# Second pass of a two-layer convolution block: spread and next normaliser placed behind the output projection, scaling of the query weights placed behind the filter's products

## The chip, the cores and the metric

The kernel runs on one core of a Trainium2 chip. The time is the device time of one execution in microseconds; the figure for the kernel before is the median of three runs. A profile is one further execution, recorded by the hardware profiler, with an own time and an own span. The engines are called as the profile calls them: PE (TensorE's matrix products), PEld (its weight loads), DVE (VectorE), ACT (ScalarE), POOL (GpSimd) and SP (SyncE, which here issues DMA transfers).

## The reference

The input x holds 8 images of 384 channels and 64 x 64 points. Two layers follow one another; each normalises over 32 groups of channels and adds its result to x. Cut to what matters:

```python
# layer 0: linear attention over the 4096 points of an image
q = apply_rope_2d(conv1x1(x, Wq, bq))
k = apply_rope_2d(conv1x1(x, Wk, bk))
v = conv1x1(x, Wv, bv)
q = elu(to_heads(q) * scale) + 1.0
k = elu(to_heads(k)) + 1.0
kv = einsum('bhnd,bhne->bhde', k, v)
k_sum = k.sum(axis=2)
normalizer = einsum('bhnd,bhd->bhn', q, k_sum)[..., None]
out = einsum('bhnd,bhde->bhne', q, kv) / (normalizer + 1e-06)
x = x + conv1x1(out, Wfc, bfc)            # of _gn(x)
# layer 1: filter in frequency space on 8x8 blocks, 3x3 depthwise, gate
t = einsum('bchw,oc->bohw', x, w_in)
t = irfft2(rfft2(blocks(t)) * fft_filter)
t = depthwise3x3(t, w_dw)
x = x + einsum('bchw,oc->bohw', gelu(t1) * t2, w_out)   # of _gn(x)
```

All sums are in 32-bit floating point.

## The kernel before

An image is cut into 8 bands of 512 points, and its 384 channels into 3 tiles of 128 partitions. An image goes through three passes. In the first, keys and values of all bands are projected and their product is summed. In the second (`queries`), the queries are projected band by band, divided by their normaliser, and multiplied by the product of the summed keys and values with the output weights; the result is added to x. In the third, layer 1 runs band by band, and between its steps the first pass of the next image is done, so that from image 1 on there is no first pass of its own. Part of the last band of layer 1 of one image (its depthwise taps, gate and contraction: `last_band`) runs inside the second pass of the next.

In the second pass a band j has these steps:

- `q_project`: 9 products of 512 columns (L655; the profile counts 18, since each is carried out as two), three for each tile of channels. Then VectorE turns and adds the biases (L667, L682, L684), ScalarE makes a part of the turned copy (L676) and the two functions of the elu (L379, L380), and VectorE ends it (L381). The function stops after each tile's products (`yield`), so that other work can be placed between them.
- `q_normalise`: 12 small products of the band's queries with the summed keys (L693, tile pn), then a chain that gives the divisor in two parts of 16 bits: on VectorE L701, L702 (reciprocal), L707 and L709, on ScalarE the casts L706 before L707 and L708 before L709. Its result is the tile `parts`.
- `q_spread`: 12 small products that spread `parts` over the channels (L717, tile prb) into four tiles, and four multiplications of the queries by them on VectorE (L726).
- `project_out`: 9 products of the queries with the folded weights (L734, tile pf; 18 in the profile), each three followed by an addition to x on VectorE (L738). After that `band_sums` forms the sums for layer 1's normalisation, on ScalarE for all bands but the first (L180, L183).

`queries` fixes the order in which these steps are written down. A scheduler then places each instruction in its engine's queue by that order, by what it depends on and by its own estimates; each engine runs its queue in order. `tc.issue_after(ins)` makes the instructions of its block stand behind `ins` in the queue, where they are on the same engine.

Within the second pass, besides, run: `late`, the rest of the image before (the taps L855 on VectorE, the gate L867 to L872, a small product L1149 whose copy L1153 holds the weights of the late taps, the contraction L888 and L899), and `chain`, which prepares the next image's key weights: its group statistics (L341 to L355 on VectorE, L348 on ScalarE, two transfers on POOL's queue that end in L359), the scaling of wk (L401) and the bias columns (L422, L426, L427).

`Keys.prepare(4)` is written down after band 4's layer 1 work in the third pass. It loads the next image's query weights wq and scales them (`scale_weight`: three instructions L401 of 384 columns on VectorE). In the built queue of the kernel before, these three stand much earlier, near the end of the second pass, between the steps L702 and L709 of band 7's divisor.

`expand_filter` is the part of layer 1 with the filter: after its products (L766) VectorE multiplies by the filter (L774, tile tf).

The lines that the change touches in `queries`, before:

```python
q_spread(b, j, q[j], normaliser.pop(j))          # j = 2 ... 7
output_ = project_out(b, j - 1, q.pop(j - 1), mt)
if j == NBAND - 2:
    next(output_)
    normalise(j + 1)
run(output_)
```

Of the kernel before, what the change touches and what calls it, by code (L numbers as in the profile page):

```python
# [15 lines left out]
C = 384  # L16
# [3 lines left out]
NBAND = 8  # L20
# [97 lines left out]
def conv_blocks_kernel(ctx: ExitStack, tc: tile.TileContext, a: dict, out: bass.AP, nb: int):  # L118
    nc = tc.nc
# [131 lines left out]
    scale = HD ** -0.5  # L251
# [147 lines left out]
    def scale_weight(w, params, factor=1.0):  # L399
        for i in range(CT):  # L400
            nc.vector.tensor_scalar(w[:, i, :], w[:, i, :], params[0][:, i : i + 1], factor, ALU.mult, ALU.mult)  # L401
# [143 lines left out]
    latest = {}  # L545
# [101 lines left out]
    def q_project(b, j, wqs, bias, q):  # L647
        tq = qp.tile([P, 4, BT], F32, tag="turn", name=f"tq_{b}_{j}")
        nc.sync.dma_start(tq, a["tq"][:, j])
        pq = [None] * CT  # L650

        for m in (2, 0, 1):
            p_ = pq[m] = ps_tile(f"pq_{b}_{j}_{m}")
            for t in range(CT):
                nc.tensor.matmul(  # L655
                    p_,
                    wqs[:, t, m * P : (m + 1) * P],
                    xt[b, j][:, t, :],
                    start=(t == 0),
                    stop=(t == CT - 1),  # L660
                )
            yield
        qc = w_tile([P, CT, BT], f"qc_{b}_{j}")
        qs = w_tile([P, CT, BT], f"qs_{b}_{j}")

        def turn(dst, src, m, table):
            nc.vector.scalar_tensor_tensor(dst, src, m, table, ALU.add, ALU.mult)  # L667

        def by_row(ap):
            return ap.rearrange("p (r w) -> p r w", w=W)  # L670

        def columns(ap):
            return ap.unsqueeze(1).to_broadcast([P, 8, W])

        for to, of in (halves, halves[::-1]):
            nc.scalar.activation(qs[to, 2, :], pq[2][of, :], AF.Identity, bias=bias[of, 2:3])  # L676
        turn(by_row(qc[:, 2, :]), by_row(pq[2]), bias[:, 2:3], columns(cq2))
        for m in range(2):
            turn(qc[:, m, :], pq[m], bias[:, m : m + 1], tq[:, 2 * m, :])
            turn(qs[:, 1 - m, :], pq[m], bias[:, m : m + 1], tq[:, 3 - 2 * m, :])  # L680
            if m == 0:
                nc.vector.tensor_mul(by_row(qs[:, 2, :]), by_row(qs[:, 2, :]), columns(sq2))  # L682
        for part in (slice(2, 3), slice(0, 2)):
            nc.vector.tensor_add(qc[:, part], qc[:, part], qs[:, part])  # L684
            elu_plus_one(qc[:, part], qs[:, part])
        q[j] = qc
# [25 lines left out]
    def q_spread(b, j, q, rn):  # L712
        pr = [ps_tile(f"prb_{b}_{j}_{s}") for s in range(4)]
        for t in range(CT):
            for s in range(4):
                strip = slice(32 * s, 32 * s + 32)
                nc.tensor.matmul(  # L717
                    pr[s][:, t * P : (t + 1) * P],
                    expand[strip, t * P : (t + 1) * P],
                    rn[strip, :],  # L720
                    start=True,
                    stop=True,
                )
        for s in range(4):
            qq = q[:, :, s * P : (s + 1) * P]
            nc.vector.tensor_mul(qq, qq, pr[s][:, :C].rearrange("p (t n) -> p t n", t=CT))  # L726
# [3 lines left out]
    def project_out(b, j, q, mt):  # L730
        for m in range(CT):
            p_ = ps_tile(f"pf_{b}_{j}_{m}")
            for t in range(CT):
                nc.tensor.matmul(  # L734
                    p_, mt[:, t, m * P : (m + 1) * P], q[:, t, :], start=(t == 0), stop=(t == CT - 1)
                )
            xm = xt[b, j][:, m, :]
            latest["sum"] = nc.vector.scalar_tensor_tensor(xm, p_, bfc[:, m : m + 1], xm, ALU.add, ALU.add).ins  # L738
            if m == 0:
                yield  # L740
        if j == 1:
            differences[b] = taps_pool.tile([P, CT, BT], F32, tag="dw", name=f"differences_{b}")
        band_sums(b, 1, j, xt[b, j], differences.get(b))


    def expand_filter(b, j, h, done):
        ht = w_tile([P, 4, C], f"ht_{b}_{j}")
        tf = w_tile([P, 4, C], f"tf_{b}_{j}")
        for i in range(4):
            p_ = ps_tile(f"pi_{b}_{j}_{i}")  # L750
            for t in range(CT):
                nc.tensor.matmul(  # L752
                    p_[:, :C],
                    h[:, t, i * P : (i + 1) * P],
                    w_in[:, t, :],
                    start=(t == 0),
                    stop=(t == CT - 1),
                )
            nc.scalar.copy(ht[:, i, :], p_[:, :C])  # L759
        yield  # L760

        for s in range(2):
            p_ = [ps_tile(f"pd_{b}_{j}_{2 * s + i}") for i in range(2)]
            for above in range(2):
                for i in range(2):
                    nc.tensor.matmul(  # L766
                        p_[i][halves[above], :C],
                        dft[halves[i], :],
                        ht[halves[i], 2 * s + above, :],
                        start=True,  # L770
                        stop=True,
                    )
            for i in range(2):
                nc.vector.tensor_mul(tf[:, 2 * s + i, :], p_[i][:, :C], filt)  # L774
        done.append(tf)

    def back_transform(b, j, tf):
# [173 lines left out]
    def run(*chains):  # L951

        chains = list(chains)
        while chains:
            chains = [c for c in chains if next(c, chains) is not chains]

    class Keys:
# [50 lines left out]
        def prepare(self, j):  # L1008

            if self.live and j == 4:  # L1010
                self.wq = load_weight(self.b, "wq", QRUNS)
                if self.b == 0:
                    sum_weight(self.wq, "wq", scale)
                scale_weight(self.wq, self.params, scale)
                if self.b == 0:
                    self.qbias = bias_columns(0, self.params[1], 2 * CT, 3 * CT)
            if self.live and j == NBAND:
                self.wfc = load_weight(self.b, "wfc", k_runs)
                if self.b == 0:
                    self.wv = load_weight(self.b, "wv", k_runs)  # L1020
                    sum_weight(self.wv, "wv")
                    bias_rows(0, bias_columns(0, self.params[1], CT, 2 * CT), CT, self.vbias)

    def queries(b, keys, before_last, late):


        wq, qbias = keys.wq, keys.qbias
        q, done, normaliser = {}, [], {}

        def normalise(j):  # L1030
            normaliser[j] = q_normalise(b, j, q[j])

        run(q_project(b, 0, wq, qbias, q))
        before_last()
        run(keys.accumulate(NBAND - 1))
        next(late, None)
        finish = keys.finish(done)
        for _ in zip(q_project(b, 1, wq, qbias, q), finish):
            pass
        prepared = []  # L1040
        chain = layer0_chain(b + 1, prepared)

        next(late, None)
        normalise(0)
        if b:
            run(finish)
        run(q_project(b, 2, wq, qbias, q))
        run(finish)
        mt = done[0]
        q_spread(b, 0, q[0], normaliser.pop(0))  # L1050
        project = q_project(b, 3, wq, qbias, q)
        next(project)
        normalise(1)
        run(project)
        run(project_out(b, 0, q.pop(0), mt))
        q_spread(b, 1, q[1], normaliser.pop(1))
        normalise(2)
        for j in range(2, NBAND):
            if j < NBAND - 2:
                project = q_project(b, j + 2, wq, qbias, q)  # L1060
                for _ in range(2):
                    next(project)
                normalise(j + 1)
                run(project)
                next(chain, None)
            q_spread(b, j, q[j], normaliser.pop(j))
            output_ = project_out(b, j - 1, q.pop(j - 1), mt)
            if j == NBAND - 2:
                next(output_)
                normalise(j + 1)  # L1070
            run(output_)
            if j < NBAND - 2:
                next(chain, None)
            if j in (5, 7):
                load_x(b + 1, j // 6)
            next(late, None)
        run(chain)
        run(project_out(b, NBAND - 1, q.pop(NBAND - 1), mt))
        return prepared
# [38 lines left out]
    filt = const.tile([P, C], F32, tag="filt", name="filt")  # L1118
# [109 lines left out]
    b = nb - 1  # L1228
# [60 lines left out]
```

## Time and profile before

| what | us |
|---|---|
| median of the runs (lowest, highest) | 3316.01 (3314.86, 3316.93) |
| profiled execution | 3317.55 |
| its span | 3315.8 |
| products L734 pf, 1152 | 510.7 |
| products L655 pq, 1152 | 521.5 |
| taps L855 on DVE, 1401 | 977.5 |
| additions L738 on DVE, 192 | 138.6 |
| granted clock of PE, mean | 0.994 |

The busy shares in the prediction are of the whole span. Where the idle time of an engine was ended by another engine's instruction, the profile names that instruction after an arrow. Lines such as L717 are those of the kernel printed above. Times in a timeline are microseconds from the span's start; an instruction's length contains some 0.08 us in which the next one on VectorE has already begun, so sums over a queue are made from start to start. In the chain of work that ended last, 90% of the span is PE, 5% DVE and 3% ACT.

### The profile page before, as it was taken

To read this page: it belongs to the slowest core of one execution; us is meant where nothing else is said; L and a number is where in the kernel's file an instruction comes from. 1 tells how busy PE (TensorE), PEld (TensorE's weight loads), DVE (VectorE), ACT (ScalarE), POOL (GpSimd) and SP (SyncE) were. 2 spreads that over 40 slices of the span, in tenths; PEclk is the share of its full clock that TensorE was granted. 3 is DMA by queue.
4 is the path that set the end of the run, shared out by engine and by line. 5 is a ranking of instruction groups with operands and counts; after the bars stand their busy time and mean duration, and the time that the engine had idled before them with its cause. 6 is when DMAs were issued, how large, how long until landed. Compare 5 with 4: busy or idle time off the path is not lost.

```text
span 3315.8 us, 53150 instructions
## 1 busy us (share of the span) xinstructions
PE 3256.2 (98%) x21133; PEld 1829.5 (55%) x21133; DVE 2755.8 (83%) x4528; ACT 2020.4 (61%) x4029; POOL 173.7 (5%) x321
## 2 busy tenths in 40 slices
PE   8999999999999999999999999999999999999988
PEld 5544666456664566545665456654566446664454
DVE  6577789978889688896889968998788987889697
ACT  4445666666766566755666656656576665556553
POOL 0000000100010000100001000010000100000000
PEclk9999999999999999999999999999999999999999
DMA  7324334462444523534335433445343551334112
GB/s 217 114 87 117 93 80 117 127 143 68 106 108 127 143 68 96 128 114 127 87 87 137 119 112 77 111 127 118 99 102 91 144 128 52 73 73 126 58 30 48
DMA packets 154446, 346.33 MB, mean 104 GB/s; under 512 B 29813, under 2 KB 41061, under 8 KB 146005
## 3 DMA queue, kind: packets, MB, share of 16 engines
q1 hardware_dynamic: 124500, 282.65, 27.0%
q0 software_dynamic: 29504, 60.06, 12.4%
q8 instruction: 166, 2.72, 0.3%
q14 instruction: 84, 0.68, 0.1%
q10 hardware_dynamic: 192, 0.21, 0.0%
HBM read 235.62 MB, written 99.93 MB: 101 GB/s over the span
## 4 chain that ended last, share of the span: by engine, by line
PE 90%; DVE 5%; ACT 3%; DMA 1%; issue 1%; SPq 0%; DVEq 0%; ACTq 0%
PE pf L734 15%; PE pk L491 14%; PE pi L752 14%; PE pv L507 13%; PE pq L655 13%; PE pw L888 5%; PE pb L787 3%; PE pw L899 3%; PE acc L523 3%; PE pd L766 3%; PE acc L536 2%; DVE dw L855 2%; PE pn L693 1%; ACT mt L570 1%; PE prb L717 1%
## 5 line engine op out<-in xcount | busy, mean ns | idle before, releaser
L855 DVE SCALAR_TENSOR_TENSOR dw<-ring,w_dw,dw 128x512 f32<-128x512 f32 x1401 | 977.5, 746 | 239.9 <-ACT ring L803 200.8
L491 PE MATMUL pk<-wk,x 128*128 128x384 f32 x1536 | 544.9, 496 | 0.0
L655 PE MATMUL pq<-x,wq 128*128 128x512 f32 x1152 | 521.5, 601 | 2.6 <-ACT mt L570 2.6
L752 PE MATMUL pi<-w_in,hf 128*128 128x384 f32 x1536 | 513.5, 491 | 1.3 <-ACT hf L374 1.3
L734 PE MATMUL pf<-qc,mt 128*128 128x512 f32 x1152 | 510.7, 597 | 0.0
L507 PE MATMUL pv<-wv,x 128*128 128x384 f32 x1344 | 470.0, 488 | 0.0
L491 PEld LDWEIGHTS pk<-wk,x 128*128 128x128 f32 x1536 | 283.5, 191 | 205.4 <-issue 32.5
L752 PEld LDWEIGHTS pi<-w_in,hf 128*128 128x128 f32 x1536 | 288.1, 190 | 195.8 <-issue 2.5
L514 ACT COPY v<-pv 128x384 f32<-128x384 f32 x224 | 108.7, 485 | 424.5 <-PE pv L507 423.2
L734 PEld LDWEIGHTS pf<-qc,mt 128*128 128x128 f32 x1152 | 214.3, 190 | 255.5 <-issue 239.6
L507 PEld LDWEIGHTS pv<-wv,x 128*128 128x128 f32 x1344 | 253.6, 190 | 181.4 <-issue 8.4
L655 PEld LDWEIGHTS pq<-x,wq 128*128 128x128 f32 x1152 | 212.8, 190 | 250.6 <-issue 226.2
L738 DVE SCALAR_TENSOR_TENSOR x<-pf,bfc,x 128x512 f32<-128x512 f32 x192 | 138.6, 744 | 81.9 <-PE pf L734 81.4
L379 ACT ACTIVATE qs<-qc 128x512 f32<-128x512 f32 (+1 forms) x128 | 107.0, 836 | 144.2 <-DVE qc L684 143.8
L180 ACT ACTIVATE differences<-x,shift 128x512 f32<-128x512 f32 x168 | 120.0, 714 | 103.8 <-DVE x L738 103.6
L888 PE MATMUL pw<-gated,w_out 128*128 128x256 f32 x768 | 179.3, 383 | 0.0
L494 DVE TENSOR_TENSOR kc<-pk,kvbias 128x384 f32<-128x384 f32 x256 | 140.7, 550 | 40.3 <-PE pk L491 40.2
L759 ACT COPY ht<-pi 128x384 f32<-128x384 f32 x256 | 115.1, 482 | 85.6 <-PE pi L752 81.8
L888 PEld LDWEIGHTS pw<-gated,w_out 128*128 128x128 f32 x768 | 146.7, 192 | 36.9 <-issue 6.9
L918 POOL DMA_DIRECT2D out_dram<-y x63 | 80.5, 1277 | 1544.6 <-DVE dw L855 799.1
L379 ACT ACTIVATE ks<-kc 128x1536 f32<-128x1536 f32 x64 | 95.0, 1485 | 95.1 <-DVE kc L498 94.8
L374 ACT ACTIVATE hf<-x,nb,rs 128x512 f32<-128x512 f32 x192 | 146.4, 808 | 2.4 <-DVE nb L319 2.3
(209 smaller groups left out, 4375.1 us busy)
## 6 DMA issues: line engine op xcount, KB each, us to landing
tq<-in_tq SPq DMA_DIRECT2D x64, 1024.0 KB, 4.9
x<-in_x SPq DMA_DIRECT2D x64, 768.0 KB, 6.1
tk<-in_tk SPq DMA_DIRECT2D x64, 768.0 KB, 4.5
out_dram<-x SPq DMA_DIRECT2D x63, 768.0 KB, 3.7
out_dram<-y POOLq DMA_DIRECT2D x63, 768.0 KB, 7.7
xs<-in_x SPq DMA_DIRECT2D x56, 768.0 KB, 5.9
dw<-tap POOLq DMA_DIRECT2D x14, 512.0 KB, 9.3
wk<-in_wk SPq DMA_DIRECT2D x8, 576.0 KB, 3.9
```

What stands on the lines that cost most here:

```text
L180: nc.scalar.activation(out[:, m, :], x_[:, m, :], AF.Identity, bias=shift[:, m : m + 1], accum_out=of_m[0])
L374: nc.scalar.activation(dst, src, AF.Identity, bias=nb_[:, t : t + 1], scale=rs[:, t : t + 1])
L379: nc.scalar.activation(e, x_, AF.Relu, scale=-1.0)
L491: nc.tensor.matmul(pk[:, :C], tokens(t), wks[:, t, :], start=(t == 0), stop=(t == CT - 1))
L494: nc.vector.tensor_add(kc[:, i, :], pk[:, :C], bias)
L507: nc.tensor.matmul(pv[:, :C], xt[b, j][:, t, i * P : (i + 1) * P], wvs[:, t, :], start=(t == 0), stop=(t == CT - 1),)
L655: nc.tensor.matmul(p_, wqs[:, t, m * P : (m + 1) * P], xt[b, j][:, t, :], start=(t == 0), stop=(t == CT - 1),)
L734: nc.tensor.matmul(p_, mt[:, t, m * P : (m + 1) * P], q[:, t, :], start=(t == 0), stop=(t == CT - 1))
L738: latest["sum"] = nc.vector.scalar_tensor_tensor(xm, p_, bfc[:, m : m + 1], xm, ALU.add, ALU.add).ins
L752: nc.tensor.matmul(p_[:, :C], h[:, t, i * P : (i + 1) * P], w_in[:, t, :], start=(t == 0), stop=(t == CT - 1),)
L855: nc.vector.scalar_tensor_tensor(acc[:, m], src, wd, acc[:, m], ALU.mult, ALU.add)
L888: nc.tensor.matmul(p_[h][:, m - m0, :], w_out[:, 0, m * P : (m + 1) * P], gated[:, h * HT : (h + 1) * HT], start=(m == m0), stop=False,)
```

## The change

In the second pass the order written down is a different one. Before, band j's spread stood before band j-1's output projection, and the normaliser product of band j+1 stood between the second and the third tile of the query products of band j+2 (for band 7: between the first and second tile of the output of band 5). After the change, the spread of band j is always followed at once by the normaliser product of band j+1; for bands 2 to 4 the two stand behind the output projection of band j-1, and for bands 5 to 7 before it. The query products of a band are no longer split, but for band 3's: its first tile's products now stand before the spread of band 0, not behind it.

For all images but the first, the scaling of wq is held behind the last multiplication by the filter that has been written down, that of band 4.

```diff
             for i in range(2):
-                nc.vector.tensor_mul(tf[:, 2 * s + i, :], p_[i][:, :C], filt)
+                latest["filtered"] = nc.vector.tensor_mul(tf[:, 2 * s + i, :], p_[i][:, :C], filt).ins
...
                 if self.b == 0:
                     sum_weight(self.wq, "wq", scale)
-                scale_weight(self.wq, self.params, scale)
+                    scale_weight(self.wq, self.params, scale)
+                else:
+                    with tc.issue_after(latest["filtered"]):
+                        scale_weight(self.wq, self.params, scale)
...
-        q_spread(b, 0, q[0], normaliser.pop(0))
         project = q_project(b, 3, wq, qbias, q)
         next(project)
-        normalise(1)
+
+        def spread(j):
+            q_spread(b, j, q[j], normaliser.pop(j))
+            if j < NBAND - 1:
+                normalise(j + 1)
+
+        def output(j):
+            run(project_out(b, j, q.pop(j), mt))
+
+        spread(0)
         run(project)
-        run(project_out(b, 0, q.pop(0), mt))
-        q_spread(b, 1, q[1], normaliser.pop(1))
-        normalise(2)
+        output(0)
+        spread(1)
         for j in range(2, NBAND):
             if j < NBAND - 2:
-                project = q_project(b, j + 2, wq, qbias, q)
-                for _ in range(2):
-                    next(project)
-                normalise(j + 1)
-                run(project)
+                run(q_project(b, j + 2, wq, qbias, q))
                 next(chain, None)
-            q_spread(b, j, q[j], normaliser.pop(j))
-            output_ = project_out(b, j - 1, q.pop(j - 1), mt)
-            if j == NBAND - 2:
-                next(output_)
-                normalise(j + 1)
-            run(output_)
+            if j < NBAND - 3:
+                output(j - 1)
+                spread(j)
+            else:
+                spread(j)
+                output(j - 1)
```

No instruction is added or left out: both kernels compute the same products and sums.

## Prediction

> **What bounds the kernel now.** I read the page's busy shares first, then TensorE's list of waits, then the second pass of image 1 in time order on TensorE and on VectorE, and last the busy table by stretch. The page:
>
> ```profile
> PE 3256.2 (98%) x21133; PEld 1829.5 (55%) x21133; DVE 2755.8 (83%) x4528; ACT 2020.4 (61%) x4029; POOL 173.7 (5%) x321
> ```
>
> TensorE is busy all but 60 us of the span, so a change can win little and lose a good deal. What TensorE waited for (total us, times, longest):
>
> ```profile
> PE pb L787 <- DVE tf L774: 14.4, 6, 3.6
> PE prb L717 <- DVE parts L709: 12.6, 14, 1.4
> ```
>
> The first row lies wholly in the last image's third pass (3161 to 3255 us), which the change does not touch. The second is the change's ground: two waits in each of images 1 to 7 (bands 0 and 2). TensorE's timeline of image 1 shows them (start, length, [idle before <- releaser]):
>
> ```profile
> 598.90 0.35 PE L717 MATMUL prb<-parts,expand 32*128 32x128 bf16 x12 [1.39 <-DVE parts L709]
> ...
> 626.28 0.35 PE L717 MATMUL prb<-parts,expand 32*128 32x128 bf16 x12 [0.41 <-DVE parts L709]
> ...
> 640.64 2.84 PE L655 MATMUL pq<-x,wq 128*128 128x512 f32 x6
> 643.42 0.35 PE L717 MATMUL prb<-parts,expand 32*128 32x128 bf16 x12
> ```
>
> ```profile
> 677.53 7.99 PE L734 MATMUL pf<-qc,mt 128*128 128x512 f32 x18
> 685.45 0.35 PE L717 MATMUL prb<-parts,expand 32*128 32x128 bf16 x12
> ...
> 698.73 0.35 PE L717 MATMUL prb<-parts,expand 32*128 32x128 bf16 x12
> ```
>
> The spreads (L717) shown are of bands 0, 2 and 3, then 6 and 7. In images 1 to 7 the spreads up to band 6 stand to within 0.02 us at the same distances behind band 0's, so one image stands for all. Now VectorE around band 6's divisor:
>
> ```profile
> 674.94 0.28 DVE L701 TENSOR_SCALAR rn<-pn 128x128 f32<-128x128 f32 x1
> ...
> 678.12 0.34 DVE L709 SCALAR_TENSOR_TENSOR parts<-part,take_off,rn 128x128 bf16<-128x128 bf16 x1
> ...
> 684.73 2.06 DVE L738 SCALAR_TENSOR_TENSOR x<-pf,bfc,x 128x512 f32<-128x512 f32 x3
> ...
> 694.69 0.32 DVE L401 TENSOR_SCALAR wq<-wq,rs 128x384 f32<-128x384 f32 x1
> ...
> 696.74 0.35 DVE L709 SCALAR_TENSOR_TENSOR parts<-part,take_off,rn 128x128 bf16<-128x128 bf16 x1
> ```
>
> Band 6's divisor (L709) ends at 678.46 and is spread at 685.45: 7.0 us to spare. Band 7's ends at 697.09, 1.6 us before its spread. The busy table by stretch (us, then PE, PEld, DVE, ACT, POOL, granted clock, DMA share, GB/s), bands 2 to 7 of the second pass and then the third pass:
>
> ```profile
> 624.00:700.00 76.00, 75.59 (x346) 34.68 (x345) 72.54 (x139) 50.87 (x107) 4.05 (x7) 1.00 0.47 113
> 730.00:990.00 260.00, 259.81 (x2053) 159.40 (x2052) 219.38 (x332) 173.62 (x348) 13.73 (x28) 1.00 0.37 99
> ```
>
> In the second pass VectorE is as full as TensorE: of its 3.5 idle us there, 2.0 come after band 7's divisor. From the first step of band 2's divisor (L701, 622.77) to the last step of band 6's (L709, 678.12) lie 55.35 us with 1.2 us idle. So a new order on VectorE's queue, not the wait on TensorE, decides what this change does.
>
> **The change on TensorE.** Nothing is added or removed; no DMA changes but for one neighbour swap each in SP's and POOL's queues in the first images (a 32-column piece of wq; a bias line), with the same work around them: priced at nothing, at most 0.1 us each. The built order becomes, for bands 2 to 4: 18 query products, 18 output products, spread, normaliser; for band 5: query, spread, normaliser of 6, output of 4, spread of 6, normaliser of 7, output of 5. Lengths from the timeline: 18 products 7.82, spread 0.28 (643.42 to 643.69), normaliser 0.79. A group of 6 between normaliser and spread takes 2.78 (640.64 to 643.42) where a third of 18 takes 2.61; a steady band takes 16.92 (643.42 to 660.33) and would take 7.82 + 7.82 + 0.28 + 0.79 = 16.71.
>
> Walked from 597.51 (end of band 2's query products) without waits: 6 products to 600.3, band 0's spread finds its divisor (ready 598.85), so the 1.39 goes; spread and normaliser to 601.4, 12 products to 606.6. The output of band 0 needs the fourth spread multiply (L726), which VectorE ends at 606.98: 0.4 of the 1.39 comes back. Then 607.0 + 7.82 + 1.07 = 615.9; two groups of 18 to 631.55 (band 2's divisor was ready at 626.4, so the 0.41 goes); 1.07 and the late weights' 0.14 to 632.8; 15.64 + 1.07 twice to 666.2; 7.82 to 674.0; 1.07 and 7.82 to 682.9. TensorE would then ask for band 6's divisor at 682.9, 2.55 before the 685.45 of today.
>
> **The change on VectorE.** The old order computed band 6's normaliser between the query products of band 7, so its divisor stood before band 7's query work. The new queue holds, from band 2's L701 to band 6's L709, 120 instructions where 105 stood. The 15 extra, by median start-to-start on this timeline: L381 twice (0.60 + 1.14), L684 twice (0.60 + 1.14), L667 0.66, four L726 (4 x 0.464), three L738 (3 x 0.661), L855 0.66, L868 0.60, L427 0.08: 9.3 us. The 105 old ones sum to 54.1 and took 55.35 with 1.2 idle, so the method holds to 0.1. The new ones sum to 63.4. The starting point does not move: from 598.50 to 622.77 VectorE has no gap, and that part of its queue is the same in both orders. Hence band 6's L709 starts no sooner than 622.77 + 63.4 = 686.17, ends 0.34 later, and its spread starts at 686.57 at the earliest, against 685.45 today.
>
> To that comes VectorE's idle time in the new order, which the trace cannot show. Lower bound 0. The nearest row has 1.2. Walking ScalarE's queue beside it gives 2.0: its band sums (L180 and L183, 0.81 + 0.61 for each of three) now come just ahead of the casts L706, and a table load (1.28) with the Gelu comes between L706 and L708 of band 3; L707 and L709 wait some 0.8 in band 3, 0.7 in band 4, and L381 some 0.3. Upper bound both, 3.2. I take 1.6, midway of 1.2 and 2.0: spread of band 6 at 688.2, after a wait of 688.2 - 682.9 = 5.3 us. Everything TensorE saved earlier is swallowed by this one wait.
>
> After it, old: 698.73 - 685.45 = 13.28 to band 7's spread; new 0.28 + 0.79 + 7.84 + 4.18 = 13.09 (0.19 less, one break fewer). Band 7's divisor is due near 695, not late. So each of images 1 to 6 loses 688.2 - 685.45 - 0.19 = 2.5 us; between 0.9 (no idle) and 4.1. Image 7 has no next image's steps: 102 instructions sum to 61.8, spread at 622.77 + 61.8 + 0.4 + 1.6 = 686.6 on image 1's scale, and 0.3 is regained behind it: +0.85 (-0.7 to +2.5). Image 0 has no late taps, and VectorE is idle 9.2 us there: from the end of band 7's query products (277.2) the queue up to band 6's L709 sums to 9.4, so 286.8, with its 0.34 and some waits 287.5 against 287.06 today, less 0.45 behind it: 0 (-1 to +1).
>
> **The scaling of wq.** Three L401 of 0.33 leave the stretch between band 7's L701 and L709. That divisor has 1.6 us to spare, so nothing is won, save 0.08 in image 0, where a 1.98 us wait for wq's load stands in that queue. They go behind the filter products of band 4 in the third pass, ahead of one key sum (L494) and the turning (L474). There VectorE idles 260 - 219.4 = 40.6 us, and that covers the 1.0 us. If that cover were gone, 7 x 1.0 = 7 us; below, -0.1.
>
> **The sum.** 6 x 2.5 + 0.85 + 0 = +16. The profiled execution took 3317.55 with a span of 3315.8; the runs' median is 3316.01. I add to the median: 3332.
>
> [...]
>
> **Rivals.** (1) TensorE alone sets the pace. For it: 98% busy, and both named waits lose their cause. Then band 6's spread comes at 682.9 and band 7's at 696.0, -2.7 in seven images and -1.1 in image 0: -20, so 3296. It decides only if VectorE reaches band 6's L709 by 682.5, 3.7 us sooner than its queue sums to; against it stands a queue that was idle 1.2 us in 55.35. A mix of this kind that ends below 3309: 0.09. (2) The order costs only its bare work: no idle on VectorE, +0.9 x 6 - 1.7 = +4, 3320. For it: ScalarE is busy 51 of 76. Against: even the old order idled 1.2. Chance of ending within 0.2% of before: 0.14. (3) A further wait: the next image's scale (L359) lands 14.75 us after L355 today (656.49 to 671.24) and holds L401 of wk in VectorE's queue; the new queue brings L355 near 655, so 669.7, and L401 to about 670.7. Each us by which it is later adds seven. With that, or with the third pass's 7 us, or idle beyond 3.2: 3345 and more, 0.07. That the change doesn't do what it says: the built queues show the moves, so no chance is left for it. The forecast itself, one of 3323 to 3345: 0.70.
>
> **Numbers.** The range reaches from idle 0 (3320) to idle 3.2 (6 x 4.1 + 2.5 + 1 = 28, 3344); with a little room below, 3319 to 3344, which leaves out the faster rival and the further wait. A measurement of this kernel tells about 0.2%, 6.6 us, from no change: faster 0.09, same 0.14, slower 0.77.
>
> **What would show it.** TensorE's wait of L717 for L709 should grow from 12.6 to about 6 x 5.3 + 4 + 1.5 = 37 us, moved from bands 0 and 2 to band 6; a new wait of L734 for L726 of some 0.4 in band 0; band 6's spread 87.9 us behind band 0's (86.55 today, and band 0's itself comes 1.4 later); the L401 of wq gone from the end of the second pass, the third pass as before. I am wrong if the wait at band 6 is under 2 us, which would mean VectorE's queue holds less before L709 than I counted, or if a new wait stands in the third pass.

## The result, and the profile after

Over six runs each, the changed kernel takes 3341.67 us (median; 3340.13 to 3342.78) and the kernel before 3316.62 (3314.86 to 3317.23): a ratio of 1.0075, 95% interval 1.0062 to 1.0088. The change costs 25 us. The profiled execution has a span of 3339.9 us, 24.1 more than before, and a mean granted clock (TensorE's clock as a share of its full speed) of 0.988 instead of 0.994.

The page, busy time by engine and then the chain that ended last:

```profile
PE 3263.0 (98%) x21133; PEld 1840.2 (55%) x21133; DVE 2755.5 (83%) x4528; ACT 2019.9 (60%) x4029; POOL 173.9 (5%) x321
...
PE 74%; DVE 18%; ACT 5%; issue 2%; DMA 0%; SPq 0%; DVEq 0%; ACTq 0%
```

The busy shares tell almost nothing: the same work, TensorE at 98% again. The chain tells more: VectorE's part of it was 5% and is 18%. What TensorE waited for (total us, times, longest):

```profile
PE prb L717 <- DVE parts L709: 26.7, 8, 3.8
...
PE pf L734 <- DVE qc L726: 3.3, 7, 0.5
```

Fourteen waits of 12.6 us together have become eight of 26.7 together, and a new small one stands at band 0's output. TensorE's timeline of image 1 shows where (start, length, [idle before <- releaser]); the spreads are those of bands 0, 3, 4, 6 and 7:

```profile
600.28 0.34 PE L717 MATMUL prb<-parts,expand 32*128 32x128 bf16 x12
...
607.30 7.99 PE L734 MATMUL pf<-qc,mt 128*128 128x512 f32 x18 [0.47 <-DVE qc L726]
...
648.88 0.35 PE L717 MATMUL prb<-parts,expand 32*128 32x128 bf16 x12
...
665.60 0.34 PE L717 MATMUL prb<-parts,expand 32*128 32x128 bf16 x12
...
674.87 0.86 PE L693 MATMUL pn<-qc,ks_bd 128*32 128x128 f32 x24
675.66 7.99 PE L734 MATMUL pf<-qc,mt 128*128 128x512 f32 x18
687.47 0.50 PE L717 MATMUL prb<-parts,expand 32*128 32x128 bf16 x12 [3.81 <-DVE parts L709]
687.90 1.51 PE L693 MATMUL pn<-qc,ks_bd 128*32 128x128 f32 x24
689.34 9.61 PE L734 MATMUL pf<-qc,mt 128*128 128x512 f32 x18
...
702.97 0.35 PE L717 MATMUL prb<-parts,expand 32*128 32x128 bf16 x12
```

Up to band 6 the change does what it is for: a steady band takes 16.72 us (665.60 - 648.88), and TensorE is ready for band 6's spread at 683.66, 1.8 us earlier than the spread stood before. There it waits 3.81 us. VectorE's timeline just ahead of the divisor it waits for:

```profile
682.59 0.29 DVE L701 TENSOR_SCALAR rn<-pn 128x128 f32<-128x128 f32 x1
...
684.31 1.31 DVE L738 SCALAR_TENSOR_TENSOR x<-pf,bfc,x 128x512 f32<-128x512 f32 x2
685.80 0.74 DVE L855 SCALAR_TENSOR_TENSOR dw<-ring,late_w,dw 128x512 f32<-128x512 f32 x1
686.46 0.69 DVE L868 TENSOR_TENSOR gated<-gated,dw 128x512 f32<-128x512 f32 x1
687.06 0.35 DVE L709 SCALAR_TENSOR_TENSOR parts<-part,take_off,rn 128x128 bf16<-128x128 bf16 x1
```

The first and the last step of one divisor, L701 and L709, stand 4.5 us apart, with three additions of the output, a tap and a gate between them. VectorE is never at rest there; it does other work first. The longer delay lies ahead of L701: the products that it reads (L693, tile pn) end at 675.73, and L701 comes 6.9 us later, behind the query work of band 7, the multiplications for band 5 and steps of the next image's weights.

The second thing to see is behind the wait. The normaliser products (L693) take 1.51 us instead of 0.86, the 18 output products 9.61 instead of 7.99. The busy table by stretch (us, then PE, PEld, DVE, ACT, POOL, granted clock, DMA share, GB/s) says why:

```profile
600.00:686.00 86.00, 83.19 (x393) 37.35 (x392) 85.12 (x160) 49.63 (x94) 3.50 (x6) 1.00 0.38 114
685.80:692.60 6.80, 5.13 (x40) 2.74 (x41) 6.64 (x14) 4.38 (x12) 0.00 (x0) 0.50 1.09 67
692.60:699.40 6.80, 6.80 (x18) 3.22 (x17) 2.86 (x6) 3.67 (x10) 0.56 (x1) 1.00 0.42 109
```

VectorE is busy 85.12 of the 86 us up to 686.00, the wait's first part among them. From 685.8 to 692.6 the granted clock is 0.50, then 1.00 again. From band 6's spread to band 7's go by 15.50 us (702.97 - 687.47); 13.28 before. The images in turn, with the wait at band 6, the half clock behind it, the stretch from band 6's spread to band 7's, and the time from band 7's spread of the image before to that of this one (402.35 before the change):

| image | wait | half clock | band 6 to 7 | from the image before |
|---|---|---|---|---|
| 0 | 1.31 | none | 8.99 | |
| 1 | 3.81 | 6.8 | 15.50 | 406.31 |
| 2 | 3.80 | 3.4 | 14.78 | 405.61 |
| 3 | 3.81 | 6.8 | 15.72 | 406.55 |
| 4 | 3.81 | 6.8 | 15.54 | 406.37 |
| 5 | 3.81 | 6.8 | 15.44 | 406.28 |
| 6 | 3.80 | 3.4 | 14.78 | 405.61 |
| 7 | 2.57 | 3.4 | 10.52 | |

Images 1 to 6 lose 22.6 us together. With image 7's 1.84, image 0's 0.26 and 0.57 won in the tail that is the span's 24.1. If a stretch at full clock takes 13.08 (the first experiment with filler shows it), 13.28 of the 22.6 lie in the slow stretches, and 1.5 in image 7's: 14.8 us for the clock, and 9.3 for the waits less what the new order saves elsewhere.

### The profile page after: what moved, and what is told of

Read it like the earlier page. It is cut to its first block, busy times and chain, and to the rows that moved or that the text cites. A ratio compares the mean times of both kernels' runs of the same rounds, so it can differ in the third digit from the quotient of the medians.

```text
span 3339.9 us, 53124 instructions
## 1 busy us (share of the span) xinstructions
PE 3263.0 (98%) x21133; PEld 1840.2 (55%) x21133; DVE 2755.5 (83%) x4528; ACT 2019.9 (60%) x4029; POOL 173.9 (5%) x321
## 4 chain that ended last, share of the span: by engine, by line
PE 74%; DVE 18%; ACT 5%; issue 2%; DMA 0%; SPq 0%; DVEq 0%; ACTq 0%
PE pk L491 14%; PE pi L752 14%; PE pv L507 13%; PE pf L734 8%; PE pq L655 5%; PE pw L888 5%; DVE dw L855 3%; PE pb L787 3%; PE pw L899 3%; PE acc L523 3%; PE pd L766 2%; DVE qc L667 2%; PE acc L536 2%; DVE qc L381 2%; DVE qc L726 2%
## 5 line engine op out<-in xcount | busy, mean ns | idle before, releaser
L734 PE MATMUL pf<-qc,mt 128*128 128x512 f32 x1152 | 517.5, 605 | 3.3 <-DVE qc L726 3.3
L655 PE MATMUL pq<-x,wq 128*128 128x512 f32 x1152 | 512.8, 599 | 2.8 <-ACT mt L570 2.8
L738 DVE SCALAR_TENSOR_TENSOR x<-pf,bfc,x 128x512 f32<-128x512 f32 x192 | 140.7, 742 | 109.9 <-PE pf L734 109.7
L759 ACT COPY ht<-pi 128x384 f32<-128x384 f32 x256 | 115.1, 482 | 86.3 <-PE pi L752 82.6
```

What stands on the lines that cost most here:

```text
L655: nc.tensor.matmul(p_, wqs[:, t, m * P : (m + 1) * P], xt[b, j][:, t, :], start=(t == 0), stop=(t == CT - 1),)
L734: nc.tensor.matmul(p_, mt[:, t, m * P : (m + 1) * P], q[:, t, :], start=(t == 0), stop=(t == CT - 1))
```

## The experiments

### The parts apart

The cuts of code show each run against the changed kernel, unless another is named. The new order alone, with wq scaled where it was:

```diff
-                    scale_weight(self.wq, self.params, scale)
-                else:
-                    with tc.issue_after(latest["filtered"]):
-                        scale_weight(self.wq, self.params, scale)
+                scale_weight(self.wq, self.params, scale)
```

> The new order of spread, normaliser and output alone; the scaling of wq as before. Theory (the queue of VectorE before band 6's divisor costs the time): the wait of L717 for L709 stays at 3.8 us in images 1 to 6 and the slow stretch behind it with it, so 3341 to 3343, as the whole change. Rival (the scaling in the third pass costs it): 3316 to 3320.

Measured: 3351.26 us, ratio 1.0104 (1.0087 to 1.0121), slower than the whole change by 9.6 by the medians and by 7.1 between the profiled spans. Neither theory expected that. VectorE's timeline of image 0 shows the place:

```profile
284.03 0.75 DVE L738 SCALAR_TENSOR_TENSOR x<-pf,bfc,x 128x512 f32<-128x512 f32 x1
292.11 0.42 DVE L401 TENSOR_SCALAR wq<-wq,rs 128x384 f32<-128x384 f32 x1 [7.33 <-DMA wq<-in_wq]
292.44 0.34 DVE L709 SCALAR_TENSOR_TENSOR parts<-part,take_off,rn 128x128 bf16<-128x128 bf16 x1
```

The scaling of the next image's wq waits 7.33 us for its load, and the divisor of band 6 is queued behind it. TensorE's spread of band 6 waits 8.40 us there (1.31 with the whole change):

```profile
292.85 0.51 PE L717 MATMUL prb<-parts,expand 32*128 32x128 bf16 x12 [8.40 <-DVE parts L709]
```

Behind the wait the spread takes 0.51 us, the normaliser products 1.51 and the 18 output products 9.08, against 0.34, 0.86 and 7.99 in image 0 of the whole change; 0.50 and 1.51 are the lengths that stand there in image 1 at a granted clock of 0.50. Band 7's spread comes at 303.73 instead of 296.66: the 7.1 us of the spans. The other 2.5 of the medians stay unexplained; the profiled execution was the fastest of its four runs.

The scaling of wq alone, in the old order (against the kernel before; `latest["filtered"]` is set as in the change):

```diff
-                scale_weight(self.wq, self.params, scale)
+                    scale_weight(self.wq, self.params, scale)
+                else:
+                    with tc.issue_after(latest["filtered"]):
+                        scale_weight(self.wq, self.params, scale)
```

> The scaling of wq alone held behind the filter's products; the old order of the second pass. Theory: 3315 to 3317, no change, and no new wait in the third pass. Rival (the scaling in the third pass costs the time): 3335 or more.

Measured: 3317.19 us, ratio 1.0000 (0.9991 to 1.0010). In the old order the edit is worth nothing, and its new place in the third pass costs nothing. In the new order it saves 7.1 us between the profiled executions, in image 0, and 9.6 by the medians.

### The clock behind the wait

Three further products of 512 columns, whose result nothing reads, between band 4's output and band 6's spread:

```diff
             else:
+                if j == 6:
+                    fill = ps_tile(f"fill_{b}")
+                    for t in range(CT):
+                        nc.tensor.matmul(
+                            fill, wq[:, t, :P], xt[b, 7][:, t, :], start=(t == 0), stop=(t == CT - 1)
+                        )
                 spread(j)
```

> The whole change, with 3 further products of 512 columns (6 in the profile, 2.6 us) between band 4's output and band 6's spread, of query weights with band 7, into a tile that nobody reads. They can only fill TensorE's wait. Theory (after 3.8 us without work TensorE is granted half its clock for 3.4 to 6.8 us, which makes the stretch to band 7's spread 15.5 us long): the wait shrinks to about 1.2, the clock stays at 1.0, the stretch takes 13.1 again, and the time falls by 6 x 2.4 + 1.6 = 16 to about 3326, though more is computed. Rival (the stretch is long for another reason: a wait for a tile, or VectorE behind): 3341 or more.

Measured: 3327.35 us, ratio 1.0029 (1.0017 to 1.0041). TensorE does more work and the kernel is 14.3 us faster than the whole change. TensorE's timeline of image 1:

```profile
687.92 0.35 PE L717 MATMUL prb<-parts,expand 32*128 32x128 bf16 x12 [1.22 <-DVE parts L709]
688.20 0.86 PE L693 MATMUL pn<-qc,ks_bd 128*32 128x128 f32 x24
688.99 7.99 PE L734 MATMUL pf<-qc,mt 128*128 128x512 f32 x18
...
701.00 0.35 PE L717 MATMUL prb<-parts,expand 32*128 32x128 bf16 x12
```

The spread comes 0.45 us later than in the whole change, and yet band 7's comes 1.97 earlier: 13.08 us at full speed, in every one of images 1 to 6. No half clock follows these waits of 1.2 us (six, 7.3 us together): in image 1 the granted clock is 1.00 from 687.50 to 697.70, and its mean over the execution is 0.994, as before the change. So the wait of the whole change cost more than its length, and the rest is the clock: 403.9 us from image to image, against 402.35 before and some 406.1 with the change.

The same with one product, which leaves a wait of 2.94 to 2.96 us in images 1 to 6 and 1.71 in image 7:

```diff
+                if j == 6:
+                    fill = ps_tile(f"fill_{b}")
+                    nc.tensor.matmul(fill, wq[:, 0, :P], xt[b, 7][:, 0, :], start=True, stop=True)
```

> The whole change with 1 further product (2 in the profile, 0.9 us) in the wait before band 6's spread instead of 3, so that 2.9 us of the wait are left in images 1 to 6 and some 1.7 in image 7. If the clock falls only where the idle time passes a bound near 2.5 (2.57 was followed by half clock for 3.4 us, 1.31 and 1.39 were not): still half clock behind most of the six, 3330 to 3342, and none in image 7. If it falls by the share of idle time in a stretch: fewer and shorter slow stretches, 3327 to 3335.

Measured: 3334.03 us, ratio 1.0052 (1.0036 to 1.0069), midway. Half clock for 3.4 us followed in images 2, 3, 5 and 6 (band 6 to 7 in 14.72 to 14.78 us) and not in 1, 4 and 7 (13.08 in images 1 and 4). Stretches of images 1 and 2 (columns as above):

```profile
687.00:690.50 3.50, 3.21 (x41) 1.83 (x42) 3.46 (x7) 3.00 (x7) 0.00 (x0) 1.00 0.20 18
1091.00:1095.00 4.00, 3.79 (x39) 2.03 (x40) 3.90 (x9) 2.93 (x7) 0.00 (x0) 0.62 0.20 23
```

The time lies in both forecast ranges; the traces decide. Waits of one length to within 0.02 us, with different results: in these runs it is not the length alone that decides. The last section sets these waits beside the times at which the granted clock changed.

### The wait itself

If VectorE's queue is the cause, band 6's divisor has to come sooner in it. One way is on TensorE, by giving the normaliser of band 6 its old place between the second and third tile of band 7's query products:

```diff
-            if j < NBAND - 1:
+            if j < NBAND - 1 and j != 5:
                 normalise(j + 1)
...
-                run(q_project(b, j + 2, wq, qbias, q))
+                project = q_project(b, j + 2, wq, qbias, q)
+                if j == 5:
+                    for _ in range(2):
+                        next(project)
+                    normalise(j + 1)
+                run(project)
```

> The whole change, but band 6's normaliser product stands between the second and third tile of band 7's query products, as it did before. Its divisor then stands at 676 on the scale of image 1 by the sum over VectorE's queue, some 6 us before TensorE asks for it. Theory: no wait at band 6, full clock, band 7's spread at about 696.2 against 698.7 in the kernel before and 703.0 in the changed one: 7 x 2.5 less than before, 3297 to 3301. Rival (VectorE's fullness makes the wait come back elsewhere, at band 5 or 7): 3310 to 3320.

Measured: 3303.39 us, ratio 0.9956 (0.9942 to 0.9971). TensorE's timeline of image 1:

```profile
670.62 0.86 PE L693 MATMUL pn<-qc,ks_bd 128*32 128x128 f32 x24
...
674.46 7.99 PE L734 MATMUL pf<-qc,mt 128*128 128x512 f32 x18
682.38 0.34 PE L717 MATMUL prb<-parts,expand 32*128 32x128 bf16 x12
...
695.56 0.35 PE L717 MATMUL prb<-parts,expand 32*128 32x128 bf16 x12
```

No wait at band 6, whose divisor's last step (L709) now stands at 675.50 on VectorE, and an image takes 400.56 us. The gain is 1.79 us an image, where some 2.5 had been expected, and the time lies above the 3297 to 3301 forecast. The 0.7 that is missing is TensorE's own path: from band 0's spread to band 6's go by 83.50 us here, and 83.38 up to the wait in the whole change, where the prediction had walked 82.6.

The other way leaves TensorE's order as the change has it and puts only band 6's divisor ahead: its four steps on VectorE, with the two casts between them on ScalarE:

```diff
         rn = small.tile(...)
+        if j == 6:
+            with tc.high_priority():
+                return divisor(b, j, pn, rn)
+        return divisor(b, j, pn, rn)
+
+    def divisor(b, j, pn, rn):
```

> The whole change with TensorE's order untouched; only the steps of band 6's divisor (L701, L702, L707, L709 and their casts) get high priority, so that they stand earlier in VectorE's queue: by its sum, band 6's L709 at 679.9 on the scale of image 1 instead of 686.1, before the 682.9 at which TensorE asks. Theory (the place in VectorE's queue is all of it): no wait at band 6, full clock, band 7's spread 96 to 97 us behind band 0's, 3297 to 3303. Rival (it is TensorE's order of the small products that costs): 3335 or more.

Measured: 3304.21 us, ratio 0.9963 (0.9950 to 0.9976). TensorE and then VectorE in image 1 (lines shifted by 6: L717 is L723, L709 is L715):

```profile
675.72 7.99 PE L740 MATMUL pf<-qc,mt 128*128 128x512 f32 x18
683.65 0.39 PE L723 MATMUL prb<-parts,expand 32*128 32x128 bf16 x12
...
696.98 0.35 PE L723 MATMUL prb<-parts,expand 32*128 32x128 bf16 x12
```

```profile
676.32 0.28 DVE L707 TENSOR_SCALAR rn<-pn 128x128 f32<-128x128 f32 x1
...
680.81 0.35 DVE L715 SCALAR_TENSOR_TENSOR parts<-part,take_off,rn 128x128 bf16<-128x128 bf16 x1
```

TensorE asks at the moment it asked in the whole change (683.65 against 683.66) and finds the divisor, 6.25 us sooner than there. 400.51 us from image to image. TensorE runs the same products in the same order, and VectorE and ScalarE the same instructions: the divisor stands earlier in their queues, and a few neighbours (multiplications L726, additions L738, ScalarE's band sums) fall behind it. That is worth 37 us against the whole change, though the time is a little above the 3297 to 3303 forecast. ScalarE's queue, which moved too, is not what the gain came from: L701 and L709 stand 4.5 us apart as in the whole change, and it is L701 that comes 6.27 us sooner (676.32 against 682.59): its input is there by 675.8 in both, and its place in VectorE's queue is what differs. That settles the cause of the wait.

Both forms were measured again, without a further edit:

> e4_six_early once more, on the chip of e5 and e6, to compare the two ways of having band 6's divisor early: 3302 to 3304; e5_six_first is 1 us faster in theory, since band 7's query products are not broken (0.16 in each image).

> e5_six_first once more, beside e9_zero_once on the same chip: 3302 to 3306, 4 to 5 us above it.

Measured: 3304.33 us, ratio 0.9962 (0.9949 to 0.9975), and 3302.82 us, ratio 0.9958 (0.9945 to 0.9972). The intervals of all four overlap; that the second form is a microsecond faster is not to be seen.

### The last small wait

On top of the second form, the four spread multiplications of band 0 (L726) put ahead as well:

```diff
+        def multiply():
+            for s in range(4):
+                qq = q[:, :, s * P : (s + 1) * P]
+                nc.vector.tensor_mul(qq, qq, pr[s][:, :C].rearrange("p (t n) -> p t n", t=CT))
+
+        if j == 0:
+            with tc.high_priority():
+                multiply()
+        else:
+            multiply()
```

> As e5_six_first, and band 0's four spread multiplications (L726) at high priority too: by the sum they end 2.5 us sooner. Theory: the wait of L734 for L726 (0.47 in each of seven images) goes, 3 us less than e5_six_first, 3294 to 3300. Rival (VectorE's fullness hands the wait on to another place): the same as e5_six_first or slower.

Measured: 3300.58 us, ratio 0.9951 (0.9936 to 0.9966). A little faster, but not by what was aimed at. Its waits of TensorE:

```profile
PE pq L655 <- DVE x L751: 5.4, 7, 0.8
```

The 0.47 us at band 0's output are gone in images 1 to 7, and 0.77 at band 4's query products have come, behind an addition that was pushed back: 400.68 us an image instead of 400.51. What it won lies in image 0, where TensorE's wait of 2.78 us at query products (for ScalarE, L570) shrank to 0.70 and the half clock behind it (0.50 from 204.53 to 207.94) went: the 12 query products take 5.42 us instead of 7.11. So the same for image 0 alone (against the version just shown):

```diff
-        if j == 0:
+        if j == 0 and b == 0:
```

> As e6_six_zero_first, but band 0's multiplications have high priority in image 0 alone. e6_six_zero_first won nothing in images 1 to 7 (0.47 before band 0's output became 0.77 before band 4's query products, 400.68 us from image to image against 400.50 in e5_six_first) and 4.4 us in image 0, where a wait of 2.8 for mt and the half clock after it are gone. If that reading holds: e5_six_first less 4.4, 3298 to 3301, 1 us less than e6_six_zero_first. If the early multiplications in images 1 to 7 did help: 3302 to 3304.

Measured: 3298.02 us, ratio 0.9945 (0.9933 to 0.9958), the fastest version here: 18.7 us under the kernel before and 43.7 under the change.

## Why the prediction was right, and where not

**The cause: shown.** That "a new order on VectorE's queue, not the wait on TensorE, decides what this change does" held: putting one divisor's chain ahead turned the sign. The waits at bands 0 and 2 went, band 0's output waits 0.47 (0.4 forecast), a steady band takes 16.72 (16.71), and band 6 waits in every image.

**The queue.** From band 2's L701 to band 6's L709 go by 64.02 us, 0.87 of them idle: 63.15 of work against 63.4 from the row sums. The idle term, 1.6, was too large: walking ScalarE's queue beside VectorE's promised holds that mostly did not come. With the start at 623.04 instead of 622.77, the spread came at 687.47, not 688.2. TensorE for its part was ready 0.76 later than walked (683.66), some 0.3 of it by band 0's output already. Hence a wait of 3.81 where 5.3 was forecast, and 26.7 us of waits in place of 37. By that sum the change would have cost 9.3 us without the clock, not 16.

**The stretch behind the wait: the step that failed.** "After it, ... new 0.28 + 0.79 + 7.84 + 4.18 = 13.09" is right at full clock (13.08 with the filler) and was 15.29 on average. The granted clock stood in the table that the prediction showed, at 1.00, and was taken to stay there. It fell to 0.50 at or behind each wait of 2.57 to 3.81 us at band 6: 14.8 us that were in no term. An overestimate of 7 and an omission of 15 make the total 24 to 25, where +16 was forecast. That the time still lies in the stated range is partly luck: the range reached that far for idle time on VectorE, which mostly did not come, and the halved clock, which no term held, filled that room; the omission alone, on top of the forecast 3332, would have ended at 3347.

**The scaling of wq: right for the old order, wrong for the new.** Priced at nothing; worth nothing alone (ratio 1.0000), but 7 us or more in the new order. The 1.98 us wait for wq's load in image 0 was seen, but priced by its place in the old queue; in the new order, left where it was, it is 7.33 us and stands ahead of band 6's divisor (the first experiment). The third pass did remain as it was: over 260 us of it TensorE is busy 259.81 us as before, and VectorE takes 0.9 more.

**The rivals.** TensorE alone setting the pace, at 3296, needed VectorE there by 682.5; it is what the two versions with band 6's divisor ahead come near to (3303); a part of what is missing is the 0.47 us an image that returns at band 0. The bare work, 3320, came nearer to the wait (3.7 us by its sum, 3.81 measured), though VectorE did idle 0.87, and knew no clock either. The further wait, by the next image's scale, did not come: L401 of wk stands at 670.14, without a wait.

## What to carry to other kernels

When an instruction is moved to spare one engine a wait, sum the queue of the engine that releases it, start to start, from a point that does not move up to the releasing instruction: here that gave the wait's place and, within 0.25 us, the queue's work. Some waits on TensorE cost more than their length here: in the changed kernel and with one or three filler products, none of the waits at band 6 of 1.2 to 1.71 us was followed by half clock, and of the 13 of 2.57 to 3.81 us 11 were. And where the releasing engine is full, the chain that is waited for has to come sooner in its queue, at the price of work that can stand back. Here that was done by an earlier product on TensorE or by putting ahead one chain of four VectorE instructions and two casts, and either way a loss of 25 us became a gain of 12 to 14.

## What the runs showed of the hardware

That the granted clock would fall was not expected. In the changed kernel the half-clock stretches at band 6's wait last 3.4 or 6.8 us, and their starts, by the trace's record of the granted clock, lie on one grid: 685.81, 1095.41, 1498.18, 1904.37, 2310.55, 2720.15 and 3122.93 are multiples of 3.413 us apart (120, 118, 119, 119, 120 and 118 of them; 2437.12 / 714 = 3.4133). So each wait can be divided among the grid's intervals. In the kernel with one filler product the starts 1091.94, 1498.13, 2307.09 and 2713.28 lie 119, 237 and 119 of the same 3.413 us apart. Three intervals of image 4 of the changed kernel (columns as in the table by stretch), the first two with the wait in them:

```profile
1900.96:1904.37 3.41, 1.19 (x3) 0.19 (x1) 3.41 (x8) 2.27 (x7) 0.44 (x1) 1.00 0.12 3
1904.37:1907.78 3.41, 1.82 (x36) 1.23 (x36) 3.38 (x8) 3.39 (x10) 0.00 (x0) 0.50 1.68 119
1907.78:1911.19 3.41, 3.41 (x8) 1.52 (x5) 3.28 (x8) 0.91 (x3) 0.00 (x0) 0.50 0.58 22
```

The idle time of TensorE in the intervals which the wait falls into:

| kernel, image | wait | idle by interval | half clock behind the first |
|---|---|---|---|
| changed, 4 | 3.81 | 2.21, 1.59 | yes |
| changed, 5 | 3.81 | 2.03, 1.78 | yes |
| changed, 7 | 2.57 | 2.52, 0.05 | yes |
| changed, 2 | 3.80 | 2.00, 1.80 | no, but behind the second |
| one filler, 2 | 2.95 | 0.27, 2.68 | no, but behind the second |
| one filler, 6 | 2.96 | 0.93, 2.02 | no, but behind the second |
| one filler, 1 | 2.94 | 1.41, 1.53 | no, nor behind the second |
| one filler, 4 | 2.94 | 1.45, 1.49 | no, nor behind the second |

In these two kernels, of the intervals at full clock that a wait at band 6 fell into, each one with 2.02 us or more of idle was followed by half clock, and none with up to 1.53. In between the traces show both: in the changed kernel's images 2 and 6 no half clock came behind the intervals with 2.00 and 1.93, and half clock came behind the next, with 1.80 and 1.87. Why there, no run shows.

What came after differs in the same way. Where an interval at half clock still held 1.23 to 1.78 us of the wait (changed kernel, images 1, 3, 4 and 5), the next one stayed at half clock, hence 6.8 us; where it held at most 0.05 (images 2, 6 and 7), full clock came back after 3.4. Elsewhere in the kernel idle time alone does not tell: in the last image's third pass of the changed kernel the interval from 3153.65, with 1.08 us of idle, was followed by half clock (0.50 from 3157.06).

From band 6's spread to band 7's go by, in images 1 to 6, 13.08 us behind the waits of 1.2 us with three filler products and behind the two of 2.94 us in images 1 and 4 with one; behind the other waits, of 2.95 to 3.81 us, 14.72 to 15.72 us, so 1.6 to 2.6 more. In images 0 and 7 of the changed kernel and image 7 with one filler product it is 8.99 us behind waits of 1.31 and 1.71 us and 10.52 behind the one of 2.57, 1.5 more.
